# Q and K computed with tokens on partitions and then transposed, against Q and K computed transposed

## The chip, the core and the metric

The kernel runs on one core of a Trainium2 chip, in one launch, on float32 data. The metric is the device time of that launch in microseconds (us). Its engines are named as in the profile: PE is TensorE (PEld its weight loads), DVE is VectorE, ACT is ScalarE, POOL is GpSimd, and SP issues the DMAs.

## The reference

The input x is 4 sequences of 512 tokens with 1024 features. One block of attention and one feed-forward block are computed, each between two layer norms, with a residual:

```
x = x + layernorm(attention(layernorm(x)))
x = x + layernorm(ffn(layernorm(x)))

attention: qkv = x @ w_qkv.T + b_qkv      # 32 query heads, 8 key/value heads, 32 wide
           q, k = rope(q), rope(k)        # pairs (even, odd) turned by the token's angle
           attn = softmax(causal(q @ k.T / sqrt(32)))
           out  = (attn @ v) @ w_o.T + b_o
ffn:       top 2 of 8 experts by x @ gate_w.T, softmax over the two
           x @ base_w.T + base_b + 2 * sum over experts of weight * (x @ A_e.T) @ B_e.T
```

## The kernel before

The 2048 tokens are 16 tiles of 128 tokens (`tok.t`), four to a sequence (`tok.i` is the place in the sequence). Tiles go through the stages in pairs. For each pair the program does: layer norm and transposes of x (`normed_x`, tiles `xa`, `pt_xn`, `T_xn`); K and V (`keys_values`, `acc_kv`); Q (`queries`, `acc_q`); attention in 88 groups of heads (`scores` into `sc`, softmax, `turn` into `pt_p`, `values` into `av`); the output product (`acc_o`, into `w`); a layer norm, residual (`y`) and second layer norm, transposes (`pt_h`, `T_h`); the gate and LoRA products (`acc_gl`, `pt_low`); and the base product (`acc_f`).

The three 1024-wide products (Q, output, base) of a pair of tiles are made with seven half-size products in place of eight (`seven`: sums `s1` to `s4` of the inputs, sums of the weights that are mixed once into DRAM, `mixed_q`, `mixed_o`, `mixed_f`). The weights arrive as 128x512 `piece` tiles in a ring of 14.

Q and K leave TensorE already transposed, features on partitions and tokens along the free axis. For Q that is `project_turned` (L612): for each piece four matmuls, a 128x128 block of the piece being the stationary operand and 128 tokens the moving one (L623). For K it is the first half of `keys_values` (L1014), 16 such matmuls for a tile of tokens; V takes 8 matmuls with 256 moving columns (L1023). `rotate` (L792) applies the rotary embedding in this layout: a VectorE `stream_shuffle` swaps the halves of each head (L805), VectorE multiplies by sin and GpSimd by cos (L803), VectorE adds (L817). Its cos and sin tables are transposed once on TensorE at the start (`rope_tables`, L845). Biases of Q and K are one value for each partition.

In the softmax (`softmax`, L1511), VectorE adds the causal mask (L1526) and takes the negated maximum (L1536) for two quadrants of four heads at a time; ScalarE takes the exponential with its sum (L1478); VectorE the reciprocal (L1507); GpSimd scales (L1492); TensorE transposes (`turn`, L1552), ScalarE or VectorE copies out (L330, L331), and TensorE multiplies by V (L1575).

The order on every engine is fixed when the program is built. An `Order` object holds a planned time for every step and the costs written in the code; `tensor` (L233) picks TensorE's next step among lanes (scores, transposes, values, and dense products last), and every other engine takes, among the operations planned to be ready, the one with the lowest `urgent` number. On the chip each engine then works through its list in order and waits where an operand is late. Slots limit what is in flight: 4 PSUM banks beside the four of `sc`, 8 soft-max tiles, 2 `xa`, 3 `y`, 14 pieces. All DMAs go through SP's one list.

A step's planned cost and what it needs look like this:

```
g.turned = [
    Step(0.109 * blocks, partial(turn, g, r), [g.normed[r]], bank=True)
    for r in range(QUADS)
]
```

The functions that the diff touches:

Of the kernel before, what the change touches and what calls it, by code (L numbers as in the profile page):

```python
# [33 lines left out]
SAFE = 0.6  # L34
# [44 lines left out]
class Step:  # L79


    def __init__(self, us, issue, needs=(), bank=False, soon=()):
        self.us, self.issue, self.needs = us, issue, list(needs) + list(soon)
        self.tiled = False
        self.piece = None
        self.bank, self.soon = bank, soon
        self.done = Task()


class Order:  # L90
    ENGINES = ("dve", "act", "pool", "sp")

    def __init__(self, banks):
        self.now = self.at = 0.0
        self.free = dict.fromkeys(self.ENGINES, 0.0)
        self.waiting = {e: [] for e in self.ENGINES}
        self.seq = 0
        self.banks = banks

# [133 lines left out]
    def tensor(self, scores, urgent, values, dense):  # L233


        while True:
# [11 lines left out]
            us = steps[0].us + TILING * steps[0].tiled  # L248
            if lane is scores and values and values[0].tiled and self._is_ready(values[0]):
                steps.append(values.pop(0))  # L250
                us = steps[0].us + steps[1].us + PAIRED
# [9 lines left out]
def kernel(  # L261
# [27 lines left out]
    BANKS, SOFT, RING = 4, 8, 14  # L289
# [6 lines left out]
    kvpool = ctx.enter_context(tc.tile_pool(name="kvpool", bufs=2))  # L296
# [12 lines left out]
    qT_slots, kT_slots, raw_slots, turn_slots = Slots(8), Slots(2), Slots(2), Slots(2)  # L309
    xa_slots, y_slots, w_slots, v_slots = Slots(2), Slots(3), Slots(4), Slots(8)  # L310
# [54 lines left out]

    bqk_sb = const.tile([P, ND + NKT], F32, name="bqk_sb")
    bv_sb = const.tile([P, KVD], F32, name="bv_sb")
    cos_sb = const.tile([P, NQ, P], F32, name="cos_sb")
    sin_sb = const.tile([P, NQ, P], F32, name="sin_sb")
# [13 lines left out]
    def loads(what):  # L383
# [16 lines left out]
    biases = {"q": bqk_sb, "o": bo_sb, "f": bbase_sb}  # L400
    bias_steps = {
        name: const.tile([P, ND // 2 if name == "q" else 512], F32, name=f"bias_step_{name}")
        for name in plain
    }
    has_bias = {name: Task() for name in plain}
# [38 lines left out]
    def bias_step(name):  # L444
        yield loaded["b", name]
        b, n = biases[name], bias_steps[name].shape[1]
        yield combine(
            4, lambda: bias_steps[name], lambda: b[:, n : 2 * n], lambda: b[:, :n], ALU.subtract
# [115 lines left out]
    def transposes(dst, src, halves, name, slot):  # L564
# [3 lines left out]
        for h in range(NH):  # L568
# [17 lines left out]
            steps.append(Step(0.44, issue, [halves[h], slot], bank=True))  # L586
# [25 lines left out]
    def project_turned(x, w, name, needs, take):  # L612


        acc = []
        steps = []

        def issue(c):
            if not acc:
                acc.append(ps.tile([P, 4, P], F32, tag="ps", name=f"acc_{name}"))  # L620
            last = c == len(needs) - 1
            for f in range(4):
                nc.tensor.matmul(  # L623
                    acc[0][:, f, :],
                    lhsT=w(c)[:, f * P : (f + 1) * P],
                    rhs=x(c),

                    start=(c == 0 and f == 0),
                    stop=last,
                    skip_group_check=True,  # L630
                )
            if last:
                start(take(acc[0], steps_of[c].done), order.now)

        for c in range(len(needs)):
            steps.append(Step(0.872, partial(issue, c), needs[c], bank=(c == 0)))
        steps_of = list(steps)
        return steps

# [6 lines left out]
    def whole(name, tok_name, k, lhsT, ready, take, room, used=None, more=None):  # L646


# [5 lines left out]
        if name == "q":  # L654
            return with_pieces(
                used,
                project_turned(
                    lambda c: lhsT()[:, c, :],
                    lambda c: used[c].sb,
                    f"{name}_{tok_name}_{k}",  # L660
                    needs,
                    take,
                ),
            )
# [14 lines left out]
    def seven(name, pair_name, tiles, ready, out, room, ended, free, more=None):  # L679
# [33 lines left out]

        def bias(what):
            if name == "q":
                return lambda: what[:, :H].unsqueeze(2).to_broadcast([P, H, P])
            return lambda: what[:, :512]

# [13 lines left out]
            (bias(biases[name]), c11, None),  # L732
            (c11, c21, None),
            (c11, c11, None),
            (bias(bias_steps[name]), c22, None),
# [7 lines left out]
        def take(k, acc, when):  # L743
# [12 lines left out]
            yield dve(0.69, 0, lambda: nc.vector.tensor_add(to(), acc, in1()))  # L756
# [9 lines left out]
        for k, (lhs, wants, of, h, half) in enumerate(blocks):  # L766
# [11 lines left out]
            def w(c, used=used, extra=extra):  # L778
                return used[c].sb if c < H else extra[1]

            label, end = f"{name}_{pair_name}_{k}", partial(take, k)
            steps += with_pieces(
                used,
                project_turned(lhsT, w, label, needs, end)
                if name == "q"
                else project(lhsT, w, 512, label, needs, end),
# [3 lines left out]
    SWAP = [(d + HD // 2) % HD for d in range(HD)]  # L790

    def rotate(raw, out, i, name):  # L792


        n = raw.shape[1]
        yield turn_slots.take()
        turn = ropes.tile([P, 4, P], F32, tag="turn", bufs=2, name=f"turn_{name}")[:, :n, :]
        cos, sin = (
            a[:, i, :].unsqueeze(1).to_broadcast([P, n, P]) for a in (cos_sb, sin_sb)
        )  # L800

        def multiply(t, by, engine):
            engine.tensor_tensor(out=t, in0=t, in1=by, op=ALU.mult)  # L803

        yield dve(0.1 + n * 0.135, 2, lambda: nc.vector.stream_shuffle(turn, raw, SWAP))  # L805

        def by_cos():
            yield pool(0.2 + n * 0.27, 1, partial(multiply, raw, cos, nc.gpsimd))

        has_cos = start(by_cos(), order.at)  # L810
        yield [loaded["sin"]]
        yield dve(0.1 + n * 0.145, 2, partial(multiply, turn, sin, nc.vector))
        yield has_cos
        yield dve(
            0.1 + n * 0.155,
            2,
            lambda: nc.vector.tensor_tensor(out=out(), in0=raw, in1=turn, op=ALU.add),  # L817
        )
        turn_slots.give(order.at)

    def rope_tables():

        def table(at, name, to):
            wide, has_wide = [], Task()

            def widen():
                yield loaded["rope"]
                yield turn_slots.take()  # L830

                def issue():
                    wide.append(ropes.tile([P, 4, P], F32, tag="turn", bufs=2, name=f"wide_{name}"))
                    nc.gpsimd.tensor_copy(
                        wide[0].rearrange("p i (r d) -> p i r d", d=HD)[:, :NQ],
                        rope_sb[:, :, at, :].unsqueeze(2).to_broadcast([P, NQ, QUADS, HD]),
                    )

                yield pool(0.9, 1, issue)
                has_wide.finish(order.at)  # L840

            def turn_table():
                pt = ps.tile([P, 4, P], F32, tag="ps", name=f"pt_{name}")
                for i in range(NQ):
                    nc.tensor.transpose(pt[:, i, :], wide[0][:, i, :], ident)  # L845

                def end():
                    yield step.done
                    turn_slots.give(order.at)
                    yield act(  # L850
# [963 lines left out]
```

## Time and profile before

| | |
|---|---|
| median of 3 runs | 1201.9 us (1200.41 to 1201.95) |
| profiled execution: its own time | 1199.83 us |
| its span, first to last instruction | 1197.7 us |
| mean granted TensorE clock | 0.992 |
| busy PE / DVE / POOL / ACT | 1144.1 / 865.8 / 638.4 / 497.1 us |
| TensorE's first instruction after the span's start | 7.49 us |
| TensorE's last matmul begins | 1187.56 us |

The span lies 2.1 us below the execution's own time, and that execution 2.1 us below the median. In the timeline a row gives the start, the time until the last of its instructions ends, engine, line, operation, output and inputs, and the number of instructions; float32 matmuls appear as two instructions each, transposes as one. Since matmuls are pipelined, the cost of a row in a run without idle time is the start of the next row less its own start.

### The profile page before, as it was taken

Reading aid. Unit: us, or ns where it says so; the run is one execution under the profiler, and the core shown is the slowest. Engines: PE = TensorE matmul, PEld = TensorE weight load, DVE = VectorE, ACT = ScalarE, POOL = GpSimd, SP = SyncE. Lnnn points to the kernel's source line nnn. Section 1 sums busy time; section 2 is a strip of 40 time slices with the busy share of each in tenths; the row PEclk is TensorE's granted clock in tenths of the full one; section 3 lists DMA queues with packets and bytes.
Section 4 is the critical chain, followed back from the end, with each engine's and each line's share of the span. In section 5 each row is a group of like instructions: output and inputs, shape, how many; then the busy total and the mean of one; then the engine's idle time right before and its main releaser. Section 6 shows DMA issues by size and latency. Waiting matters only on the chain.

```text
span 1197.7 us, 24865 instructions
## 1 busy us (share of the span) xinstructions
PE 1144.1 (96%) x8976; PEld 796.1 (66%) x8976; DVE 865.8 (72%) x1704; ACT 497.1 (42%) x1447; POOL 638.4 (53%) x874
## 2 busy tenths in 40 slices
PE   6999899999799999999999999999999999979996
PEld 6988757875468855687658885577855875545443
DVE  4787878886677866888677886677766796777353
ACT  1335344543445344454345544444444533454110
POOL 2566857653656545555376654555555563554321
PEclk9999999999999999999999999999999999999999
DMA  9568769555572547715587234761558545733783
GB/s 325 207 237 303 262 227 317 206 180 168 185 232 88 175 157 246 214 66 165 158 260 231 93 124 142 254 208 47 172 187 277 178 150 177 255 106 119 250 304 102
DMA packets 119626, 232.10 MB, mean 194 GB/s; under 512 B 14800, under 2 KB 15952, under 8 KB 119504
## 3 DMA queue, kind: packets, MB, share of 16 engines
q1 hardware_dynamic: 119504, 230.51, 58.7%
q8 instruction: 72, 1.18, 0.4%
q14 instruction: 50, 0.41, 0.1%
HBM read 209.49 MB, written 20.97 MB: 192 GB/s over the span
## 4 chain that ended last, share of the span: by engine, by line
PE 75%; DVE 10%; POOL 7%; ACT 3%; issue 2%; DMA 2%; SPq 0%; POOLq 0%; ACTq 0%; DVEq 0%
PE acc_f L600 18%; PE acc_o L600 15%; PE acc_q L623 12%; PE pt_p L1552 10%; PE sc L1457 6%; PE av L1575 5%; POOL pr L1492 3%; DVE nmax L1536 3%; PE acc_kv L1014 3%; PE acc_kv L1023 3%; ACT pr L1478 2%; PE acc_gl L600 2%; POOL qT L803 1%; DVE sc L1526 1%; PE pt_xn L575 1%
## 5 line engine op out<-in xcount | busy, mean ns | idle before, releaser
L1492 POOL TENSOR_SCALAR pr<-pr,rtot 128x256 f32<-128x256 f32 (+3 forms) x512 | 304.1, 609 | 266.6 <-DVE rtot L1507 208.2
L1478 ACT ACTIVATE pr<-sc,nmax 128x256 f32<-128x256 f32 (+3 forms) x512 | 264.7, 531 | 204.8 <-DVE nmax L1536 96.6
L1536 DVE TENSOR_REDUCE nmax<-sc 128x2 f32<-128x768 f32 (+3 forms) x176 | 198.0, 1125 | 61.4 <-ACT pr L1478 60.0
L330 ACT COPY prT<-pt_p 128x512 f32<-128x512 f32 (+1 forms) x206 | 109.4, 543 | 227.1 <-PE pt_p L1552 226.3
L1552 PE MATMUL pt_p<-ident,pr 128*128 128x128 f32 x1280 | 180.4, 278 | 18.8 <-POOL pr L1492 13.7
L1552 PEld LDWEIGHTS pt_p<-ident,pr 128*128 128x128 f32 x1280 | 143.1, 140 | 70.2 <-issue 33.1
L331 DVE COPY prT<-pt_p 128x512 f32<-128x512 f32 (+1 forms) x146 | 94.0, 645 | 40.6 <-PE pt_p L1552 39.2
L623 PE MATMUL acc_q<-T_xn,piece 128*128 128x128 f32 x896 | 108.7, 278 | 2.1 <-DMA piece<-in_w_qkv_dram 2.1
L600 PE MATMUL acc_f<-piece,T_h 128*128 128x512 f32 x232 | 109.7, 598 | 0.4 <-ACT prT L330 0.4
L623 PEld LDWEIGHTS acc_q<-T_xn,piece 128*128 128x128 f32 x896 | 105.7, 195 | 5.7 <-issue 5.3
L623 PE MATMUL acc_q<-s_q,piece 128*128 128x128 f32 x896 | 109.0, 276 | 0.4 <-ACT prT L330 0.3
L600 PE MATMUL acc_o<-piece,s_o 128*128 128x512 f32 x224 | 103.5, 601 | 3.6 <-POOL s_o L338 3.6
L1478 ACT ACTIVATION_READ_ACCUMULATOR pr<-sc,nmax 128x1 f32 x512 | 106.0, 207 | 0.0
L623 PEld LDWEIGHTS acc_q<-s_q,piece 128*128 128x128 f32 x896 | 104.4, 192 | 1.5 <-ACT prT L330 0.8
L600 PE MATMUL acc_o<-piece,aT 128*128 128x512 f32 x232 | 104.4, 593 | 0.0
L600 PE MATMUL acc_f<-piece,s_f 128*128 128x512 f32 x224 | 103.6, 594 | 0.4 <-POOL s_f L338 0.4
L1526 DVE TENSOR_TENSOR sc<-sc,cmask 128x256 f32<-128x256 f32 (+2 forms) x176 | 96.4, 548 | 10.4 <-ACT pr L1478 5.3
L1575 PEld LDWEIGHTS av<-prT,v 128*32 128x32 f32 x2560 | 65.3, 110 | 51.6 <-issue 42.1
L1457 PE MATMUL sc<-kT,qT 32*128 32x384 f32 (+3 forms) x1024 | 93.9, 464 | 0.6 <-DVE qT L817 0.5
L1575 PE MATMUL av<-prT,v 128*32 128x128 f32 x2560 | 90.4, 276 | 1.3 <-ACT prT L330 1.0
L338 POOL TENSOR_TENSOR y<-y,w 128x512 f32<-128x512 f32 x62 | 78.8, 1286 | 22.6 <-ACT w L550 19.9
L525 POOL TENSOR_TENSOR rstd<-veps,neg_half 128x1 f32<-128x1 f32 x64 | 36.8, 579 | 101.3 <-DVE veps L521 100.3
(159 smaller groups left out, 1522.6 us busy)
## 6 DMA issues: line engine op xcount, KB each, us to landing
piece<-in_w_o_dram SPq DMA_DIRECT2D x116, 256.0 KB, 3.9
piece<-in_w_base_dram SPq DMA_DIRECT2D x116, 256.0 KB, 3.2
piece<-mixed_q SPq DMA_DIRECT2D x112, 256.0 KB, 3.7
piece<-mixed_o SPq DMA_DIRECT2D x112, 256.0 KB, 4.1
piece<-mixed_f SPq DMA_DIRECT2D x112, 256.0 KB, 3.2
piece<-in_w_qkv_dram SPq DMA_DIRECT2D x100, 256.0 KB, 3.8
xa<-in_x_dram SPq DMA_DIRECT2D x32, 256.0 KB, 3.4
y<-in_x_dram SPq DMA_DIRECT2D x16, 512.0 KB, 5.1
```

The costliest lines, as they stand in the source:

```text
L330: act=(0.15 + n * 0.00085, lambda: nc.scalar.copy(out(), in_())),
L331: dve=(0.15 + n * 0.00105, lambda: nc.vector.tensor_copy(out(), in_())),
L338: engine.tensor_tensor(out=out(), in0=in0(), in1=in1(), op=op)
L600: nc.tensor.matmul(acc[0][:, :n], lhsT=lhsT(c), rhs=w(c), start=(c == 0), stop=last)
L623: nc.tensor.matmul(acc[0][:, f, :], lhsT=w(c)[:, f * P : (f + 1) * P], rhs=x(c),  start=(c == 0 and f == 0), stop=last, skip_group_check=True,
L1457: nc.tensor.matmul(sc[:, r, c * n : (c + 1) * n], lhsT=tok.qT[g.kt][rows, (g.at + c) % GROUP, :], rhs=seq.kT[rows, g.kt, :n], start=True, ...
L1478: lambda: nc.scalar.activation(pr[:, c * n : (c + 1) * n], sc4[:, r, c, :], AF.Exp, bias=nmax[:, r, c : c + 1], accum_out=total[:, r, c : ...
L1492: lambda: nc.gpsimd.tensor_scalar(pr[:, c * n : (c + 1) * n], pr[:, c * n : (c + 1) * n], rtot[:, r, c : c + 1], 1.0, ALU.mult, ALU.mult,),
L1526: lambda: nc.vector.tensor_tensor(out=diag, in0=diag, in1=cmask.unsqueeze(1).unsqueeze(1).to_broadcast([P, q, g.n, P]), op=ALU.add,),
L1536: lambda: nc.vector.tensor_reduce(nmax[:, some, : g.n], sc4[:, some], AX.X, ALU.max, negate=True),
L1552: nc.tensor.transpose(pt[:, j, :], g.pr[r][:, j * P : (j + 1) * P], ident)
L1575: nc.tensor.matmul(av[r * HD : (r + 1) * HD, c, :], lhsT=g.seq.v[j][:, head * HD : (head + 1) * HD], rhs=g.prT[r][:, c * (i + 1) + j, :], ...
```

## The change

Q and K are now computed as the other products are: 128 tokens are the stationary operand and 512 columns of weights (for K and V together, 512 columns of `wkv_sb`) the moving one. The result has tokens on partitions. The bias becomes a row that is broadcast to all partitions (`bqkv_sb`, 768 KB of DMA in place of a small one and 128 KB). `rotate` works in this layout, with the halves of a head swapped by addressing: two VectorE multiplications by sin, one of GpSimd by cos, one VectorE addition. Then TensorE transposes: four 128x128 blocks for each Q tile of 512 columns (32 tiles, `pt_q`), two for each K tile (16 tiles, `pt_k`), and ScalarE (Q, with the scale) or ScalarE or VectorE (K) copies out. The two table transposes at the start are gone, and so is the shuffle.

To make room for six `raw` tiles, `xa` has one buffer in place of two, `y` two in place of three, the ring 13 pieces in place of 14; K has four separate tiles.

In the order, the turn of an even quadrant now waits in the plan until the odd one beside it is scaled too; masks and maxima have urgency 0 (1 before) and the sums that take a product of `seven` out of PSUM have urgency 1 (0 before). The planner adds 0.05 us where transposes follow other work, and its margin `SAFE` is 0.3 in place of 0.6. The diff, cut to its core (removed bodies stand in the functions above):

```diff
-SAFE = 0.6
+TURNING = 0.05
+SAFE = 0.3
...
+            us += TURNING * (steps[0].turns and not self.turned)
+            self.turned = steps[0].turns
...
-    BANKS, SOFT, RING = 4, 8, 14
+    BANKS, SOFT, RING = 4, 8, 13
...
-    kvpool = ctx.enter_context(tc.tile_pool(name="kvpool", bufs=2))
+    kvpool = ctx.enter_context(tc.tile_pool(name="kvpool", bufs=4))
...
-    qT_slots, kT_slots, raw_slots, turn_slots = Slots(8), Slots(2), Slots(2), Slots(2)
-    xa_slots, y_slots, w_slots, v_slots = Slots(2), Slots(3), Slots(4), Slots(8)
+    qT_slots, kT_slots, raw_slots, turn_slots = Slots(8), Slots(4), Slots(6), Slots(1)
+    xa_slots, y_slots, w_slots, v_slots = Slots(1), Slots(2), Slots(4), Slots(8)
...
-    bqk_sb = const.tile([P, ND + NKT], F32, name="bqk_sb")
-    bv_sb = const.tile([P, KVD], F32, name="bv_sb")
-    cos_sb = const.tile([P, NQ, P], F32, name="cos_sb")
-    sin_sb = const.tile([P, NQ, P], F32, name="sin_sb")
+    bqkv_sb = const.tile([P, QKV], F32, name="bqkv_sb")
...
-            steps.append(Step(0.44, issue, [halves[h], slot], bank=True))
+            steps.append(Step(0.44, issue, [halves[h], slot], bank=True, turns=True))
...
-    def project_turned(x, w, name, needs, take):
...
-            yield dve(0.69, 0, lambda: nc.vector.tensor_add(to(), acc, in1()))
+            yield dve(0.69, 1, lambda: nc.vector.tensor_add(to(), acc, in1()))
...
-                project_turned(lhsT, w, label, needs, end)
-                if name == "q"
-                else project(lhsT, w, 512, label, needs, end),
+                project(lhsT, w, 512, f"{name}_{pair_name}_{k}", needs, partial(take, k)),
...
-    def rotate(raw, out, i, name):
...
+    def rotate(raw, n, i, name):
+        nh, half = n // HD, HD // 2
         yield turn_slots.take()
+        turn = ropes.tile([P, 512], F32, tag="turn", name=f"turn_{name}")
+        raw3, turn3 = (a[:, :n].rearrange("p (h d) -> p h d", d=HD) for a in (raw, turn))
+        for a, b in ((0, half), (half, 0)):
+            sin = rope_sb[:, i, 1, a : a + half].unsqueeze(1).to_broadcast([P, nh, half])
+            yield dve(
+                0.1 + n * 0.00065,
+                2,
+                lambda: nc.vector.tensor_tensor(
+                    out=turn3[:, :, a : a + half],
+                    in0=raw3[:, :, b : b + half],
+                    in1=sin,
+                    op=ALU.mult,
+                ),
+            )
+        cos = rope_sb[:, i, 0, :].unsqueeze(1).to_broadcast([P, nh, HD])
+        yield pool(
+            0.2 + n * 0.0021,
+            1,
+            lambda: nc.gpsimd.tensor_tensor(out=raw3, in0=raw3, in1=cos, op=ALU.mult),
         )
         yield dve(
+            0.1 + n * 0.0012,
             2,
+            lambda: nc.vector.tensor_add(raw[:, :n], raw[:, :n], turn[:, :n]),
         )
         turn_slots.give(order.at)
-    def rope_tables():
...
+    def new_raw(name):
+        return ropes.tile([P, 512], F32, tag="raw", bufs=6, name=f"raw_{name}")
...
-        job.xn = xpool.tile([P, D], F32, tag="xa", bufs=2, name=f"xa_{job.name}")
+        job.xn = xpool.tile([P, D], F32, tag="xa", bufs=1, name=f"xa_{job.name}")
...
-            tok.y = xpool.tile([P, D], F32, tag="y", bufs=3, name=f"y_{tok.t}")
+            tok.y = xpool.tile([P, D], F32, tag="y", bufs=2, name=f"y_{tok.t}")
...
+        def take(acc, done):
+            yield done
             job.read(order.at)
+            yield loaded["b", "q"]
             def v_issue():
                 seq.v[i] = kvpool.tile([P, KVD], F32, tag="v", bufs=8, name=f"v_{t}")
+                nc.vector.tensor_add(
+                    seq.v[i], acc[:, KVD : 2 * KVD], bqkv_sb[:, D + KVD : D + 2 * KVD]
+                )
             yield dve(0.41, 0, v_issue)
+            seq.has_v[i].finish(order.at)
+            raw.append(new_raw(f"k_{t}"))
+            yield dve(
+                0.1 + KVD * 0.00115,
+                0,
+                lambda: nc.vector.tensor_add(
+                    raw[0][:, :KVD], acc[:, :KVD], bqkv_sb[:, D : D + KVD]
+                ),
+            )
             banks.give(order.at)
+            yield from rotate(raw[0], KVD, i, f"k_{t}")
+            k_ready.finish(order.at)
+        def turn_k():
+            pt = ps.tile([P, 4, P], F32, tag="ps", name=f"pt_k_{t}")
+            for kt in range(NKT):
+                nc.tensor.transpose(pt[:, kt, :], raw[0][:, kt * P : (kt + 1) * P], ident)
+            def end():
+                yield step_k.done
+                raw_slots.give(order.at)
+                for kt in range(NKT):
+                    yield copy(
+                        P,
+                        lambda: seq.k_tile(kt)[:, i * P : (i + 1) * P],
+                        lambda: pt[:, kt, :],
+                    )
+                banks.give(order.at)
+                seq.has_k[i].finish(order.at)
+            start(end(), order.now)
+        step_k = Step(0.23, turn_k, [k_ready], bank=True, turns=True)
+        needs = [[job.ready[c // 4], loaded["kv", c]] for c in range(ND)]
+        needs[0] += [has_raw]
+        products = project(
+            lambda c: job.xnT()[:, c, :], lambda c: wkv_sb[:, c, :], 2 * KVD, f"kv_{t}", needs, take
+        )
+        return [step_k], products
...
+        def ended(k, h):
+            yield from rotate(raw[k, h], 512, pair[k].i, f"q_{pair[k].t}_{h}")
+            q_ready[k, h].finish(order.at)
+        def turn_q(k, h):
             tok = pair[k]
+            pt = ps.tile([P, 4, P], F32, tag="ps", name=f"pt_q_{tok.t}_{h}")
+            for c in range(4):
+                nc.tensor.transpose(pt[:, c, :], raw[k, h][:, c * P : (c + 1) * P], ident)
+            def end():
+                yield steps_q[k, h].done
+                raw_slots.give(order.at)
                 tok.qT[h] = qpool.tile([P, 4, P], F32, tag="qT", name=f"qT_{tok.t}_{h}")
+                yield act(
+                    0.6, 0, lambda: nc.scalar.activation(tok.qT[h], pt, AF.Copy, scale=QSCALE)
+                )
+                banks.give(order.at)
+                tok.has_q[h].finish(order.at)
+            start(end(), order.now)
+        for k, h in [(0, 0), (0, 1), (1, 0), (1, 1)][: NH * len(pair)]:
+            q_ready[k, h] = Task()
+            steps_q[k, h] = Step(0.44, partial(turn_q, k, h), [q_ready[k, h]], bank=True, turns=True)
+        names = [q_job[tok] for tok in pair]
         if len(pair) == 2:
...
+            return [[steps_q[0, 0], steps_q[0, 1]], [steps_q[1, 1]], [steps_q[1, 0]]], steps
...
                     0.15 + q * g.n * 0.135,
-                    1,
+                    0,
...
                     0.15 + q * g.n * n * 0.00105,
-                    1,
+                    0,
...
+        bias_q = load(("b", "q"), 768, bqkv_sb, b_qkv.broadcast_to([P, QKV]))
...
-            yield from loads([rotary] + biases_qkv)
+            yield from loads([bias_q, rotary])
...
-            Step(0.109 * blocks, partial(turn, g, r), [g.normed[r]], bank=True)
+            Step(0.109 * blocks, partial(turn, g, r), [g.normed[r | 1]], bank=True, turns=True)
```

## The prediction

> **What bounds the kernel now.** I read first the page's busy times, its chain that ended last, and busy time by stretches of the span, then TensorE's timeline, then the groups by shape.
>
> ```profile
> PE 1144.1 (96%) x8976; PEld 796.1 (66%) x8976; DVE 865.8 (72%) x1704; ACT 497.1 (42%) x1447; POOL 638.4 (53%) x874
> ...
> PE 75%; DVE 10%; POOL 7%; ACT 3%; issue 2%; DMA 2%; SPq 0%; POOLq 0%; ACTq 0%; DVEq 0%
> ```
>
> TensorE is the bound: 1144.1 of 1197.7 us. Of the other 53.6 us, 7.5 pass before its first instruction and about 9 after its last matmul (1187.56 plus 1.02 us); some 37 us are waits between. So two numbers decide: how much TensorE work the change adds, and what becomes of the 37. Stretches of the span (length, then busy time of PE, PEld, DVE, ACT, POOL, then the granted clock):
>
> ```profile
> 50.00:160.00 110.00, 100.42 (x985) 87.24 (x983) 90.48 (x151) 46.14 (x152) 81.39 (x103) 1.00 0.68 237
> 310.00:330.00 20.00, 13.64 (x144) 7.96 (x139) 12.39 (x22) 11.09 (x43) 14.44 (x22) 0.91 0.51 172
> 1055.00:1100.00 45.00, 36.67 (x325) 24.30 (x317) 34.63 (x71) 22.31 (x68) 24.41 (x39) 0.92 0.24 74
> 1073.00:1076.00 3.00, 1.55 (x6) 1.18 (x7) 1.93 (x7) 2.96 (x17) 2.09 (x5) 0.50 0.00 0
> 1076.00:1079.00 3.00, 3.00 (x10) 2.08 (x10) 0.96 (x2) 1.33 (x8) 3.00 (x6) 0.50 0.00 0
> ```
>
> The waits sit in three places: 9.6, 6.4 and 8.3 us, 24 of the 37. The last two rows show a second cost: after the longest wait the clock is granted at 0.50 for 6 us, which loses 3 us more. TensorE's timeline:
>
> ```profile
> 321.71 5.40 PE L600 MATMUL acc_o<-piece,s_o 128*128 128x512 f32 x8 [3.61 <-POOL s_o L338]
> 326.94 1.45 PE L600 MATMUL acc_o<-piece,aT 128*128 128x512 f32 x3
> ...
> 399.77 3.74 PE L623 MATMUL acc_q<-T_xn,piece 128*128 128x128 f32 x32
> 403.34 1.88 PE L600 MATMUL acc_f<-piece,T_h 128*128 128x512 f32 x4
> ...
> 413.06 2.84 PE L1014 MATMUL acc_kv<-T_xn,wkv_sb 128*128 128x128 f32 x24
> 415.74 1.89 PE L1023 MATMUL acc_kv<-wkv_sb,T_xn 128*128 128x256 f32 x8
> ...
> 1044.52 1.96 PE L1552 MATMUL pt_p<-ident,pr 128*128 128x128 f32 x16
> 1046.32 7.03 PE L600 MATMUL acc_o<-piece,s_o 128*128 128x512 f32 x16
> ...
> 1073.67 1.08 PE L575 MATMUL pt_h<-ident,w 128*128 128x128 f32 x4 [4.94 <-DVE w L544]
> ...
> 1180.69 7.03 PE L600 MATMUL acc_f<-piece,T_h 128*128 128x512 f32 x16
> 1187.56 1.02 PE L600 MATMUL acc_f<-wlora_sb,lowT 128*128 128x512 f32 x2
> ```
>
> Start to start in unbroken runs: a 512-column matmul (two instructions) takes 2 x 6.87/16 = 0.859 us. The 128-column Q form takes 3.57/32 = 0.112 us an instruction, 0.893 us for the eight of a piece. A transpose takes 1.80/16 = 0.1125 us. The eight instructions at 321.71 take 5.23 us in place of 3.44: 1.8 us lost to the slower clock after a wait.
>
> **TensorE work, part by part.** Q has 228 pieces (2 tiles x 16, then 7 pairs x 28). In the new form each saves 0.893 - 0.859 = 0.034 us: 7.8 us. K and V of a tile: now 32 instructions of 0.112 (2.68/24) and 16 V instructions of 0.216 (the first tile's V: 3.45 us from 20.23 to 23.68 for 16), 7.03 us; after, eight matmuls of 0.859, 6.87. Over 16 tiles: 2.6 us saved. Added: 32 x 4 + 16 x 2 = 160 transposes, less 8 of the tables, 152 x 0.1125 = 17.1 us. In the changed program's fixed order on TensorE, 73 scores are followed directly by values, 77 before; a break costs about 0.1 us more: 0.4. Sum: 17.1 - 7.8 - 2.6 + 0.4 = 7.1 us more work on the bound. No other engine can hide it.
>
> One rule weighs on this. The row says 0.1125 us for a transpose, at a granted clock of 1.00. The Trainium skill (TensorE: Matmul & The Clock Gate, Part 4) says that transposes do not count as activity for the clock gate and gives about 275 ns for one in a kernel; by that the 152 would cost 42 us and the change would lose some 32. Its figure equals the page's mean length of one transpose record, which is not the spacing; the row decides.
>
> **The other engines.** Groups by shape (mean ns after the busy time):
>
> ```profile
> L805 DVE STREAM_SHUFFLE turn_q<-qT 128x512 f32<-128x512 f32 x32 | 23.4, 733 | 0.0
> L803 DVE TENSOR_TENSOR turn_q<-turn_q,sin_sb 128x512 f32<-128x512 f32 x32 | 31.7, 994 | 0.3
> L1478 ACT ACTIVATION_READ_ACCUMULATOR pr<-sc,nmax 128x1 f32 x512 | 106.0, 207 | 0.0
> L1478 ACT ACTIVATE pr<-sc,nmax 128x128 f32<-128x128 f32 x128 | 45.1, 385 | 24.1 <-DVE nmax L1536 13.8 <-DVE sc L1526 10.3
> ```
>
> VectorE per Q tile loses a shuffle (0.733) and a full multiplication (0.994) and gains two of half the size: 0.35 each if dense, 0.62 (K's 256-element multiplication, 624 ns) if the strided form is slow; I take 0.5. That is 0.7 x 32 = 23 us less on VectorE (15 to 33); K adds a 0.42 bias sum and two copies of about 0.28, some 10 us back. ScalarE gains 32 copies of 0.59 and loses 32 of 0.37. At 72% and 42% busy both stay off the bound, so these count nothing by themselves. GpSimd's cos product stays at 1.475 us.
>
> **The waits.** The order of TensorE's instructions is fixed in both programs, so I counted the TensorE work (at the spacings above) that stands between a producer and its consumer. Before, each big wait is where that cover is short. Near 312 us: 7.4 us from a group's scores to its first turn, then no work between the last `av` and the product that needs `s_o`. Near 149 to 156 us: 5.5 and 8.2 us from scores to turn. Near 1063 us: 6.3 and 7.0. After, the shortest such cover anywhere is 7.9 us, most are 8.6 to 13, and `s_o` has 6.1 us. What it must cover, for a 512-wide group: mask 0.43, maximum 1.22, two exponentials at 0.69 + 0.21, reciprocal 0.16, scaling 0.76: 4.4 us, up to about 9 where VectorE and ScalarE are shared. So:
> - 310 to 330 us: 6.4 + 1.8 us now, 0.6 left: -7.6.
> - 50 to 160 us: 9.6 now. The first groups (one block of keys) stay short: 16 exponentials of 0.385 + 0.207 are 9.5 us, and their cover is 14.4 and 15.5 against 14.2 and 16.8. Others gain 1 to 5 us of cover. 5 left: -4.6.
> - 1055 to 1100 us: 8.3 + 3 now. The last such group has 11.5 us of cover, where the same kind waited at 14.2; and the first `pt_h` behind it needs ScalarE after its exponentials. 8 left: -3.3.
> - Start: the 2.07 us wait for the first piece of Q goes, since K and V's weights, loaded ahead, are used first; the 768 KB bias row (2.4 us at the 322 GB/s of that stretch) delays later pieces: -1.
> - New: 48 turns of Q and K, each behind a VectorE and GpSimd chain. For K it is 0.42 + 0.42 + two products + 0.81 + 0.57, about 3 to 3.5 us, and the cover is 3.6 to 4.3 at five of 16; for Q 4.5 to 6 us with covers of 5.2 up: 0 to 10 us, near the low end: +1.8.
>
> Three edits I cost at nothing. Masks ahead of sums: a sum (0.69) waits at most 1.65 us behind them, with its PSUM bank and whoever needs that; uncovered, a few tenths each. Turns in twos: the first turn starts one scaling (0.45 to 0.76) later under dense work, and the second is 0.45 later than it need be, which is what GpSimd's lateness (13.7 us over 17 waits at L1552) is made of; gain 0 to 7, counted above. Fewer buffers: a tile's x can be asked for only after the turns of the one before, in SP's one list, with pieces behind it; the shortest distance is 10.2 us of TensorE work against about 8 for load, statistics and scaling; 0 to 3 us lost once.
>
> Sum: -7.6 - 4.6 - 3.3 - 1 + 1.8 = -14.7 of waits, +7.1 of work: -7.6. On the profiled execution 1199.8 - 7.6 = 1192.2; it lies 2.1 below the median, so 1194.3 against 1201.9.
>
> **Rivals.**
> *Slower:* the new turns themselves. TensorE works in order, so a turn that comes before its rotated tile stops everything behind it. At 0.8 us (the mean wait at L1552 on GpSimd) over half of the 48, 19 us come back, and 1194.3 - 1.8 + 19 = 1211. It decides from a mean of about 0.25 us over all 48 (12 us), where the gain is gone. For: VectorE's products share time with GpSimd (0.994 against the 0.69 of single rows early on). Against: nearly all covers exceed the chains. Chance 0.31, centred at 1208.
> *No change:* the order covers better but late engines move the waits, 8 of the 14.7 us are found: 1201. Chance 0.11.
> *Better:* the last stretch clears as well and turns cost nothing: 1184. Chance 0.10.
> *Forecast as reckoned:* 0.48, 1188 to 1199.
>
> **The numbers.** 0.2% of 1201.9 is 2.4 us, about what a measurement of this kernel can tell from no change. Faster (under 1199.5): 0.48 + 0.10 = 0.58. Within: 0.11. Slower (over 1204.3): 0.31. The range runs from 1184, the better case, to 1211, the slower rival's price; beyond lie some 2 in 10.
>
> **What would show it.** Right: TensorE's busy time up by 5 to 9 us, PE idle between its first and last matmul near 22 us, no stretch with a lowered clock between 100 and 1000 us, `acc_q` at 0.43 us an instruction. Wrong: idle above 32 us; many waits at `pt_q` or `pt_k` on VectorE's last addition; waits on DMA in the first 100 us; a transpose spacing far over 0.1125.

## The result and the profile after

The changed kernel takes 1189.0 us (median of 4 runs, 1187.5 to 1189.7) against 1201.9: a ratio of 0.9892, 95% interval 0.9875 to 0.9910. The profiled execution took 1187.52 us with a span of 1185.7, 12.0 us less than before. The direction was forecast, and the time lies in the range as reckoned, 5 us below its middle.

The page after, busy times and the chain that ended last:

```profile
PE 1145.5 (97%) x7248; PEld 627.0 (53%) x7248; DVE 823.9 (69%) x1609; ACT 533.1 (45%) x1555; POOL 608.0 (51%) x857
...
PE 80%; DVE 8%; DMA 4%; POOL 4%; ACT 2%; issue 1%; SPq 0%; POOLq 0%; ACTq 0%; DVEq 0%
```

TensorE's share of the chain rises from 75% to 80%. VectorE is busy 42 us less, three times the 13 that the prediction had, which will matter below. The same stretches as before (length, busy time of PE, PEld, DVE, ACT, POOL, then the granted clock):

```profile
50.00:160.00 110.00, 103.15 (x693) 56.58 (x694) 84.47 (x148) 54.38 (x171) 75.50 (x104) 1.00 0.76 266
310.00:330.00 20.00, 19.29 (x112) 10.63 (x113) 14.66 (x19) 12.26 (x47) 15.25 (x26) 1.00 0.70 220
1055.00:1100.00 45.00, 38.67 (x261) 23.71 (x260) 27.99 (x66) 14.47 (x50) 20.45 (x35) 0.92 0.43 143
```

At 310 to 330 us TensorE idled 6.4 us before and 0.7 now, and the clock stays at 1.00. In the other two places 6.9 and 6.3 us are left, of 9.6 and 8.3. The waits that remain, in TensorE's timeline:

```profile
59.05 0.63 PE L996 MATMUL pt_q<-ident,raw_q 128*128 128x128 f32 x4 [1.51 <-DVE raw_q L771]
...
317.04 3.67 PE L602 MATMUL acc_o<-piece,s_o 128*128 128x512 f32 x8 [0.71 <-PE av L1490]
...
1070.61 2.23 PE L577 MATMUL pt_h<-ident,w 128*128 128x128 f32 x8 [5.90 <-DVE rtot L1422]
```

The product with `s_o` now waits 0.71 us, not 3.61; one long wait, near 1070 us, is still there; and some of the new turns of Q wait for VectorE's last addition (1.51 us here, 1.27 at 107.36).

For sums over the whole span I count as **work** each row of TensorE's timeline at the spacing of its kind in unbroken runs (0.430 us for an instruction with 512 columns, 0.110 for a transpose, and so on) with what a change of kind costs; what is left between starts is **waits**, the loss to a slow clock included. Before: 1124.3 work, 56.6 waits. After: 1132.0 and 37.3. With 0.5 us less ahead of the first instruction, that is 7.7 - 19.3 - 0.5 = -12.1, the 12.0 of the span. How the sum is split depends on what is counted as a change of kind: with the commonest spacing of each pair of instructions every kernel has 13 to 16 us less work and as much more waits, and differences to the kernel before move by up to some 2 us.

### The profile page after: what moved, and what is told of

Read it like the earlier page. It is cut to its first block, busy times and chain, and to the rows that moved or that the text cites. A ratio compares the mean times of both kernels' runs of the same rounds, so it can differ in the third digit from the quotient of the medians.

```text
span 1185.7 us, 21412 instructions
## 1 busy us (share of the span) xinstructions
PE 1145.5 (97%) x7248; PEld 627.0 (53%) x7248; DVE 823.9 (69%) x1609; ACT 533.1 (45%) x1555; POOL 608.0 (51%) x857
## 4 chain that ended last, share of the span: by engine, by line
PE 80%; DVE 8%; DMA 4%; POOL 4%; ACT 2%; issue 1%; SPq 0%; POOLq 0%; ACTq 0%; DVEq 0%
PE acc_f L602 19%; PE acc_o L602 15%; PE acc_q L602 11%; PE pt_p L1467 11%; PE acc_kv L602 7%; PE sc L1372 6%; PE av L1490 6%; PE acc_gl L602 2%; DVE nmax L1451 2%; POOL pr L1407 2%; ACT pr L1393 1%; PE pt_h L577 1%; DVE sc L1441 1%; DMA mix_o<-in_w_o_dram 1%; PE pt_q L996 1%
## 5 line engine op out<-in xcount | busy, mean ns | idle before, releaser
L1467 PE MATMUL pt_p<-ident,pr 128*128 128x128 f32 x1280 | 174.2, 276 | 3.5 <-POOL pr L1407 1.6
L335 ACT COPY prT<-pt_p 128x512 f32<-128x512 f32 (+1 forms) x264 | 135.2, 548 | 83.6 <-PE pt_p L1467 82.9
L602 PE MATMUL acc_kv<-wkv_sb,T_xn 128*128 128x512 f32 x256 | 119.4, 600 | 0.0
L335 ACT COPY aT<-av 128x128 f32<-128x128 f32 (+2 forms) x82 | 25.6, 312 | 195.0 <-PE av L1490 195.0
L1393 ACT ACTIVATION_READ_ACCUMULATOR pr<-sc,nmax 128x1 f32 x512 | 108.9, 213 | 0.0
L602 PE MATMUL acc_q<-piece,s_q 128*128 128x512 f32 x224 | 105.1, 597 | 1.2 <-DVE raw_q L713 0.9
L602 PE MATMUL acc_q<-piece,T_xn 128*128 128x512 f32 x224 | 102.7, 594 | 0.0
L336 DVE COPY prT<-pt_p 128x512 f32<-128x512 f32 (+1 forms) x88 | 56.2, 641 | 32.2 <-PE pt_p L1467 31.5
```

What stands on the lines that cost most here:

```text
L335: act=(0.15 + n * 0.00085, lambda: nc.scalar.copy(out(), in_())),
L336: dve=(0.15 + n * 0.00105, lambda: nc.vector.tensor_copy(out(), in_())),
L602: nc.tensor.matmul(acc[0][:, :n], lhsT=lhsT(c), rhs=w(c), start=(c == 0), stop=last)
L1393: lambda: nc.scalar.activation(pr[:, c * n : (c + 1) * n], sc4[:, r, c, :], AF.Exp, bias=nmax[:, r, c : c + 1], accum_out=total[:, r, c : ...
L1467: nc.tensor.transpose(pt[:, j, :], g.pr[r][:, j * P : (j + 1) * P], ident)
```

## The experiments

The change has two halves: the new layout of Q and K, with its buffers, and three edits of the order: masks and maxima ahead of sums ("masks", which is two urgencies: masks and maxima from 1 to 0, and sums from 0 to 1), turns in twos ("twos"), and the planner's costs ("margin": `SAFE`, with the 0.05 of `TURNING` in the kernels with 0.3 or 0.4 except e11). In the expectations theory A is that the order's edits make the gain and the layout costs time; theory B that the layout makes it. All times are medians of 4 to 10 runs, against 1202.4, 1202.5 and 1202.7 us for the kernel before in the three sessions. Work and waits are those of each profiled execution.

| kernel | layout | order edits | time, us | ratio to before, 95% | work | waits |
|---|---|---|---|---|---|---|
| before | old | none | 1201.9 | 1 | 1124.3 | 56.6 |
| e12 | old | margin 0.5 | 1200.0 | 0.9968 to 0.9993 | 1124.6 | 58.3 |
| e11 | old | margin 0.3 | 1204.0 | 1.0003 to 1.0027 | 1125.1 | 63.6 |
| e10 | old | twos | 1204.2 | 0.9999 to 1.0022 | 1123.5 | 62.4 |
| e5 | old | masks | 1185.1 | 0.9845 to 0.9875 | 1124.5 | 44.4 |
| e8 | old | masks, margin 0.3 | 1177.7 | 0.9776 to 0.9809 | 1124.4 | 36.8 |
| e1 | old | masks, margin 0.3, twos | 1187.0 | 0.9863 to 0.9893 | 1126.3 | 42.4 |
| e2 | new | none | 1207.4 | 1.0028 to 1.0065 | 1131.0 | 55.4 |
| e4 | new | margin 0.3, twos | 1192.7 | 0.9911 to 0.9959 | 1131.4 | 40.0 |
| e6 | new | masks, twos | 1189.6 | 0.9874 to 0.9928 | 1131.3 | 37.7 |
| e3 | new | masks, margin 0.3 | 1181.7 | 0.9819 to 0.9850 | 1130.7 | 31.6 |
| e9 | new | masks, margin 0.4 | 1188.6 | 0.9857 to 0.9895 | 1131.2 | 39.7 |
| after | new | masks, margin 0.3, twos | 1189.0 | 0.9875 to 0.9910 | 1132.0 | 37.3 |
| e7 | new | as after, Q's turns doubled | 1196.0 | 0.9927 to 0.9960 | 1145.3 | 31.7 |

### The two halves apart

**e1: the order's edits on the kernel before.** Edits to its program, all three (the lines by which the planner adds `TURNING` left out):

```diff
-SAFE = 0.6
+TURNING = 0.05
+SAFE = 0.3
...
-            yield dve(0.69, 0, lambda: nc.vector.tensor_add(to(), acc, in1()))
+            yield dve(0.69, 1, lambda: nc.vector.tensor_add(to(), acc, in1()))
...
                     0.15 + q * g.n * 0.135,
-                    1,
+                    0,
...
                     0.15 + q * g.n * n * 0.00105,
-                    1,
+                    0,
...
-            Step(0.109 * blocks, partial(turn, g, r), [g.normed[r]], bank=True)
+            Step(0.109 * blocks, partial(turn, g, r), [g.normed[r | 1]], bank=True, turns=True)
```

> The kernel before with the three edits of the order alone (turns in twos, masks and maxima ahead of the sums of the seven products, the planner's margin 0.3 and 0.05 per turn); Q and K stay computed transposed, buffers as before. Theory A, the order edits took the waits away and the layout only costs 7.3 us of TensorE work: the waits fall by about 19 us as in the changed kernel and the work stays, so 1182 us. Theory B, the layout took the waits away (VectorE is 42 us less busy), the order edits are worth little: 1199 to 1203. Theory C, every new plan moves the waits by some us without a single cause: anywhere from 1188 to 1206.

**e2: the new layout with the order of before.** The same lines taken back in the changed kernel (margin 0.6, no `TURNING`, masks 1, sums 0, `g.normed[r]`):

```diff
-TURNING = 0.05
-SAFE = 0.3
+TURNING = 0.0
+SAFE = 0.6
...
-            Step(0.109 * blocks, partial(turn, g, r), [g.normed[r | 1]], bank=True, turns=True)
+            Step(0.109 * blocks, partial(turn, g, r), [g.normed[r]], bank=True, turns=True)
```

> The changed kernel with the three order edits undone: layout and buffers of the change, order rules of before. Theory A: work up by 7.3 us, waits as before: 1209 us. Theory B: the waits stay low: 1187 to 1191. Theory C: 1188 to 1206, and not the mirror image of the first run.

Measured: 1187.0 and 1207.4. The order's edits alone bring the whole gain; the layout alone is slower by 0.3 to 0.65%. Theory B falls. The layout's long wait is where it was; stretches and timeline of e2:

```profile
310.00:330.00 20.00, 15.61 (x132) 9.66 (x129) 11.09 (x16) 8.68 (x37) 14.53 (x25) 0.85 0.44 141
```

```profile
308.84 0.83 PE L1467 MATMUL pt_p<-ident,pr 128*128 128x128 f32 x4 [1.95 <-POOL pr L1407]
309.60 2.09 PE L1372 MATMUL sc<-kT,qT 32*128 32x128 f32 x32
...
319.76 5.21 PE L602 MATMUL acc_o<-piece,s_o 128*128 128x512 f32 x8 [3.61 <-POOL s_o L343]
```

It is the wait of before to the digit, 3.61 us for `s_o`.

### Which of the order's edits

**e3: without twos**, and **e4: without masks**, each from the changed kernel:

```diff
-            Step(0.109 * blocks, partial(turn, g, r), [g.normed[r | 1]], bank=True, turns=True)
+            Step(0.109 * blocks, partial(turn, g, r), [g.normed[r]], bank=True, turns=True)
```

> The changed kernel with turns planned one quadrant at a time again. If the twos carry part of the gain: TensorE's waits for GpSimd at the turns of the probabilities go from 1.7 us back towards 13.7, so 1195 to 1201. If they carry none: 1187 to 1191. Theory C: within 6 us of 1189 on either side with the change in waits spread over the span.

```diff
-            yield dve(0.69, 1, lambda: nc.vector.tensor_add(to(), acc, in1()))
+            yield dve(0.69, 0, lambda: nc.vector.tensor_add(to(), acc, in1()))
...
                     0.15 + q * g.n * 0.135,
-                    0,
+                    1,
...
                     0.15 + q * g.n * n * 0.00105,
-                    0,
+                    1,
```

> The changed kernel with masks and maxima at urgency 1 and the sums of the seven products at urgency 0 again. If masks first carry part of the gain: scores wait longer for VectorE, waits return where the cover is short, 1193 to 1200. If none: 1187 to 1191.

Measured: 1181.7 without twos, outside all its expectations, and 1192.7 without masks. Taken out of the changed kernel, masks cost 3.7 us and twos gain 7.3; both are within the scatter between orders that e9 shows below, so neither is clear from these two runs. And 3.7 us is far from the 18 that the three make in this layout, so the next runs took them one at a time in the old one.

**e5: masks alone on the kernel before.**

```diff
-            yield dve(0.69, 0, lambda: nc.vector.tensor_add(to(), acc, in1()))
+            yield dve(0.69, 1, lambda: nc.vector.tensor_add(to(), acc, in1()))
...
                     0.15 + q * g.n * 0.135,
-                    1,
+                    0,
...
                     0.15 + q * g.n * n * 0.00105,
-                    1,
+                    0,
```

> The kernel before, with only the urgencies changed: masks and maxima first, sums behind them. Theory A (the three order edits each have an effect of their own, and the effects add up): masks first took 3.7 us off the changed kernel, so 1198 to 1199 here against 1202. Rival N (any edit of a planned cost or an urgency gives a new order whose time is a draw with a scatter of several us): anything from 1195 to 1209, with no relation to the 3.7.

Measured: 1185.1, 17 us less, far outside either expectation: masks alone bring more than the whole change does. The stretch of 310 to 330 us, and TensorE's timeline there:

```profile
310.00:330.00 20.00, 19.88 (x165) 10.98 (x164) 13.99 (x25) 11.76 (x46) 18.91 (x35) 1.00 0.78 257
```

```profile
312.32 1.17 PE L1457 MATMUL sc<-kT,qT 32*128 32x128 f32 x32
...
316.22 1.02 PE L600 MATMUL acc_f<-wlora_sb,lowT 128*128 128x512 f32 x2
...
317.95 3.60 PE L600 MATMUL acc_o<-piece,aT 128*128 128x512 f32 x8
...
322.49 3.70 PE L600 MATMUL acc_o<-piece,s_o 128*128 128x512 f32 x8
```

No wait is left. TensorE's order itself is another one: dense `acc_f` work is still in hand until 317 us, while before it was used up at 306, and only output products and groups of heads followed up to 331. The timeline of before, there:

```profile
305.04 1.02 PE L600 MATMUL acc_f<-wlora_sb,lowT 128*128 128x512 f32 x2
305.89 3.60 PE L600 MATMUL acc_o<-piece,aT 128*128 128x512 f32 x8
```

The urgencies thus moved far more than VectorE's list. They also moved work between engines. The groups that copy the turned soft-max out of PSUM, before and then e5 (the number after x is the count):

```profile
L330 ACT COPY prT<-pt_p 128x512 f32<-128x512 f32 (+1 forms) x206 | 109.4, 543 | 227.1 <-PE pt_p L1552 226.3
L331 DVE COPY prT<-pt_p 128x512 f32<-128x512 f32 (+1 forms) x146 | 94.0, 645 | 40.6 <-PE pt_p L1552 39.2
```

```profile
L331 DVE COPY prT<-pt_p 128x512 f32<-128x512 f32 (+1 forms) x84 | 53.4, 638 | 35.8 <-PE pt_p L1552 34.8
```

With masks first, the planner gives 62 more of these copies to ScalarE, and VectorE's time in them falls by 41 us. VectorE as a whole loses 24 (865.8 to 842.0), since it takes over other work: the additions of L338 on it go from 90 to 120, and GpSimd is busy 31 us less. The split of the copies goes with masks in every kernel: VectorE makes 81 to 93 of them in the eight kernels with masks first, and 144 to 156 in the six without. In the changed kernel this group is 38 us shorter on VectorE (94.0 to 56.2), which is most of the 42.

**e6: the changed kernel with the planner's costs of before.**

```diff
-TURNING = 0.05
-SAFE = 0.3
+TURNING = 0.0
+SAFE = 0.6
```

> The changed kernel with the planner's costs of before (margin 0.6 in place of 0.3, no 0.05 for the first turn); masks first and turns in twos stay. Theory A, adding up: all order edits together are worth 18 us in the new layout, masks first 3.7 of them, twos cost 7, so the margin is worth about 21: 1208 to 1212. Rival N: 1185 to 1200. If waits grow, they should be waits of TensorE for VectorE at the places 310 to 330 and 1055 to 1100 us.

Measured: 1189.6. Margin and `TURNING` do nothing beside masks and twos; adding up fails.

**e8: masks and margin on the kernel before.** Against e1:

```diff
-            Step(0.109 * blocks, partial(turn, g, r), [g.normed[r | 1]], bank=True, turns=True)
+            Step(0.109 * blocks, partial(turn, g, r), [g.normed[r]], bank=True)
```

> The kernel before (Q and K made transposed) with masks first and the planner's new costs, but without turns in twos. Theory A, adding up: 1187 with all three, less the 7 us that twos cost in the new layout: 1178 to 1182, the shortest of all, since the layout's 152 transposes are not there. Rival N: 1182 to 1195. Rival L (the new layout is what makes the order without twos good): above 1187.

Measured: 1177.7, the fastest of all, 11 us under the changed kernel. It keeps the old layout, and its waits (36.8) are as few as the changed kernel's. Against e1 it has no twos, and its soft-max turns don't carry the planned 0.05.

**e10: twos alone on the kernel before; e11: margin 0.3 alone; e12: margin 0.5 alone.**

```diff
-            Step(0.109 * blocks, partial(turn, g, r), [g.normed[r]], bank=True)
+            Step(0.109 * blocks, partial(turn, g, r), [g.normed[r | 1]], bank=True)
```

> The kernel before, with turns in twos alone. Theory A (twos cost time by themselves): 1207 to 1212. Rival S (twos and masks first stand in for each other: either takes away the waits where VectorE is late, and together they give little more): 1188 to 1196.

```diff
-SAFE = 0.6
+SAFE = 0.3
```

> The kernel before, with the planner's margin 0.3 in place of 0.6 and nothing else. Theory A (masks first is what the gain needs; the margin only adds to it): 1198 to 1204. Rival S2 (the margin alone takes away the long waits): 1188 to 1196, and no wait near 310 to 330 us.

```diff
-SAFE = 0.6
+SAFE = 0.5
```

> The kernel before with the margin at 0.5 in place of 0.6: an order made anew from nearly the same costs, which measures the scatter between orders. Theory A: 1200 to 1205, so that differences of 7 us and more between kernels mean something. Rival N (every order is a draw): as far as 1190 or 1210.

Measured: 1204.2, 1204.0, 1200.0: e10 in neither of its expectations, e11 and e12 in those of theory A. Four orders of the old layout without masks lie within 4.2 us; three with masks lie at 1177.7, 1185.1 and 1187.0. The step between the two sets is larger than the scatter in either, so in the old layout masks are the cause: alone (e5) and with the others (e1, e8) they bring the gain, and without them twos and margin, each alone, do not. e12's timeline still shows the wait for `s_o`, a little later:

```profile
329.38 5.95 PE L600 MATMUL acc_o<-piece,s_o 128*128 128x512 f32 x8 [3.61 <-POOL s_o L338]
```

**e9: e3 with margin 0.4.**

```diff
-SAFE = 0.3
+SAFE = 0.4
```

> The changed kernel without turns in twos, and with the planner's margin at 0.4 in place of 0.3, to give another order of the same kind. Theory A (turns in twos cost 7 to 9 us, whatever the order): 1179 to 1185, near the 1181.7 of margin 0.3. Rival N (the 7 us are a lucky order): 1186 to 1192.

Measured: 1188.6, where 0.3 gave 1181.7, as rival N expected. A change of 0.1 in a planned margin moves the time by 7 us, as much as taking twos out did. Twos cost 7 us (after against e3), 9.3 (e1 against e8, with the 0.05), and 1.5 or nothing in e10; whether that is twos or the scatter between orders stays open.

### The price of the transposes

**e7: each of Q's transposes made twice**, the plan being the same:

```diff
-            for c in range(4):
+            for c in [0, 1, 2, 3, 0, 1, 2, 3]:
                 nc.tensor.transpose(pt[:, c, :], raw[k, h][:, c * P : (c + 1) * P], ident)
```

> The changed kernel with each of Q's 128 transposes made twice in a row, the second over the first (the planned order is unchanged). Theory A (the new transposes lie on the path of TensorE at 0.11 us each): 128 x 0.1104 = 14.1 us more, 1203. Rival W (TensorE would wait at these places anyway for the rotated tile or a bank, so that transposes are partly free): less than 8 us more, under 1197. By the Trainium skill's figure of some 275 ns for a transpose it would be 35 us, 1224.

Measured: 1196.0, 7.0 us more for 128 transposes, half of what they take, and so under the 8 us of rival W. The work is there (128 at 0.109 us, start to start, are 14.0 us; 13.3 more in the table), but waits fall from 37.3 to 31.7; of the fall 3.6 us are idle time ahead of the turns of Q and K (8.5 to 4.9). One such place, in e7's timeline, beside the first row of after's shown above:

```profile
58.67 1.06 PE L996 MATMUL pt_q<-ident,raw_q 128*128 128x128 f32 x8 [0.46 <-DVE raw_q L771]
```

The wait of 1.51 us has become 0.46. Behind two doubled turns TensorE comes to this place 0.67 us later (58.21 in place of 57.54), and VectorE had that much more time; the tile was also ready 0.38 us sooner, which the run does not explain. So the work added here cost its length less the waits that it covered later. The layout points the same way in the table: at equal order edits it adds about 6 to 7 us of work, but only 5.0 (before, e2), 4.0 (e8, e3) and 2.0 us (e1, after) of time. These are differences between orders too, and within their scatter.

## Why the prediction was right, and where it was not

| step | predicted | measured in the profiled executions, counted by spacing |
|---|---|---|
| TensorE work | +7.1 | +7.7 |
| 310 to 330 us | -7.6 | -8.1 |
| 50 to 160 us | -4.6 | -4.1 |
| 1055 to 1100 us | -3.3 | -3.5 |
| start | -1 | -2.5 |
| all other waits, the new turns among them | +1.8 | -1.5 |
| sum | -7.6 | -12.0 |

**Work.** Right within 0.6: Q's products at 0.43 us an instruction, transposes at 0.11, and 128 transposes doubled cost 0.055 us each in time and 0.11 in work (e7). The Trainium skill's some 275 ns for a transpose (TensorE: Matmul & The Clock Gate, Part 4) would have made that 35 us; the measurement decides against it. (The prediction's loss of 32 us by this figure is its work alone; with the 14.7 us of waits it would have been 17.) Nor does its other statement hold here, that transposes don't count as activity: in e4 TensorE ran nothing but 16 transposes, 3.14 us of work, from 1075.86 to 1079.27 at a clock of 0.50, and then the clock was 1.00.

TensorE's busy time, which I had named as the sign (5 to 9 us more), rose by 1.4 only. It also counts what the lowered clock adds, by an estimate 3.0 us less after than before (half of the 5.8 and 11.9 us of its busy time at 0.50); the other 3 us of the difference stay open. It was a poor sign, and start-to-start spacing the better one. The other signs came: 24.0 us idle between the first and the last matmul (22 named), no lowered clock between 100 and 1000 us, `acc_q` at 0.43 us an instruction.

**The three places.** Counted by spacing, each is within 0.6 us of the forecast. The forecast itself was made in idle time and loss to the clock, and in these the stretches shown lose 7.5, 2.7 and 2.0 us (5.7 idle and 1.8 of the clock; 2.7; 2.0, at a clock of 0.92 before and after): only the first is near. And from 50 to 160 us the agreement is luck in either count. The soft-max turns, whose cover I had counted, wait 8.5 us there before and 1.7 after, more of a gain than the 4.6 that I took; the new turns wait 4.9 us in the same stretch, where I had put 1.8 for all of them, in a row of its own. The two errors cancel. These turns between 50 and 162 us, in before, e5, e2 and after (busy, mean ns, then idle time ahead of them):

```profile
L1552 PE MATMUL pt_p<-ident,pr 128*128 128x128 f32 x120 | 19.4, 283 | 8.5 <-POOL pr L1492 8.5
L1552 PE MATMUL pt_p<-ident,pr 128*128 128x128 f32 x126 | 20.2, 287 | 8.1 <-POOL pr L1492 8.1
L1467 PE MATMUL pt_p<-ident,pr 128*128 128x128 f32 x113 | 16.2, 280 | 0.6 <-POOL pr L1407 0.6
L1467 PE MATMUL pt_p<-ident,pr 128*128 128x128 f32 x116 | 16.6, 278 | 1.7 <-POOL pr L1407 1.3 <-ACT qT L1003 0.4
```

The covers were read from the changed program's fixed order, which held all edits at once.

**The cause.** Here a step failed: "Three edits I cost at nothing. Masks ahead of sums: a sum (0.69) waits at most 1.65 us behind them". I priced what the edit does to two neighbours in VectorE's list. The urgency is an input of the planner, and with it the order of TensorE and the split of copies between engines change; e5 shows the edit to be worth 17 us alone. The covers that I counted held its work with that of the other edits, and the sum came out because they were counted, not because the edit was understood. The places do not all belong to it: at 310 to 330 us masks alone leave no wait (e5) and the layout alone leaves 3.61 us for `s_o` (e2), but at 50 to 162 us masks alone leave the soft-max turns at 8.1 us and the layout alone at 0.6 (there a wait of 5.2 us of the scores for ScalarE comes in their place). VectorE's relief was likewise put on the wrong account: the layout alone (e2) takes 8 us off it, and some 15 if the ten more copies that it makes there are left out, near my 13 (a half product took 0.53 us there for my 0.5); most of the 42 is copies.

**Turns in twos** ("gain 0 to 7, counted above"): the wait that I meant does go: TensorE waits 6.9 us for GpSimd's scaling in e8 and 0.7 in e1. The time does not: work and waits together are 7.5 us more in e1. In no pair of runs here did this edit gain time.

**The missing 5 us.** The gain at the start was under-sized by 1.5. The new turns' +1.8 was under-sized too: they did wait, and more than I allowed: 8.5 us of idle time in these two groups of after (busy, mean ns, then idle time ahead of them), of which 6.2 on VectorE's last addition:

```profile
L996 PE MATMUL pt_q<-ident,raw_q 128*128 128x128 f32 x128 | 19.6, 277 | 6.9 <-DVE raw_q L771 4.6 <-DVE rank L1163 1.3 <-DVE rtot L1422 0.9
L945 PE MATMUL pt_k<-ident,raw_k 128*128 128x128 f32 x32 | 6.4, 283 | 1.6 <-DVE raw_k L771 1.6
```

That is 0.18 us on a mean turn, under the 0.25 from which the slower rival would have decided. What I had left out is on the other side: the soft-max turns wait 3.5 us in all, and 18.8 before, over the whole span and not in three places alone; between 600 and 1055 us all waits together fall by 5.7. The groups, before and after:

```profile
L1552 PE MATMUL pt_p<-ident,pr 128*128 128x128 f32 x1280 | 180.4, 278 | 18.8 <-POOL pr L1492 13.7 <-ACT prT L330 1.9 <-DVE T_xn L331 1.3
```

```profile
L1467 PE MATMUL pt_p<-ident,pr 128*128 128x128 f32 x1280 | 174.2, 276 | 3.5 <-POOL pr L1407 1.6 <-DVE prT L336 0.4 <-ACT qT L1003 0.4
```

**The rivals.** The slower one described a true mechanism at a third of its price. The better one (1184) expected the last stretch to clear; it did not, in any kernel. That the layout alone is slower was in none of them: no rival took the two halves apart. So the time was right, and the gain was credited to a change whose larger half costs time.

**Open.** Masks alone in the new layout were not run, nor the two urgencies of "masks" one without the other. And e4, without masks, is still 14.7 us faster than e2, so in that layout twos and margin stand in for them in part; how, the runs do not show. Whether masks work by VectorE's order, by the copies or by TensorE's order is not separated either: the planner changes all three.

## What to carry to other kernels

Where a planner builds the order, a number in it is no local edit: run it alone on the old kernel before crediting its gain to the change that came with it, and run two or three neighbours of it to learn the scatter between orders (here some 4 to 7 us). Count waits from the finished order of the changed program, and look at who waits in a stretch as well as how long: one of the three counts here was right by two errors that cancelled. Price added work on the bound at its length less the waits that it covers later (14 us cost 7 in e7). Here the layout is the half to leave out: the old one with masks first and the smaller margin takes 1177.7 us, 2.1% less than before (interval 1.9 to 2.2%); a neighbouring order may lie some us off that.

## What was not expected of the hardware

- **The clock changed on a fixed grid, so the place of a wait on it counted.** In e2 the wait of 1.95 us at 308.84 is followed by 32 score matmuls in 2.02 us start to start (309.60 to 311.62), with a granted clock of 0.57 from 308.8 to 311.6. Before, 1.89 us at 312.39 is followed by the same 32 in 1.10 us (312.98 to 314.08), at a clock of 1.00. In each of the 14 traces all changes of the granted clock lie whole steps of 3.41 us apart (before: at 321.88, 325.29 and, 149 steps behind the first, 830.46). On this grid e2's wait lies in one step, which holds 1.46 us of TensorE work, and the next step runs at 0.50; the wait of before is cut in two by a border at 311.64, its steps hold 2.27 and 2.66 us, and the clock stays. Two steps of e2, then two of before:

```profile
305.78:309.19 3.41, 1.46 (x36) 1.17 (x36) 2.72 (x7) 2.12 (x6) 1.10 (x2) 1.00 0.95 299
309.19:312.60 3.41, 3.41 (x40) 2.86 (x39) 0.33 (x3) 0.58 (x1) 2.36 (x5) 0.50 0.38 145
308.23:311.64 3.41, 2.27 (x35) 1.01 (x34) 2.32 (x6) 1.92 (x5) 0.00 (x0) 1.00 0.70 200
311.64:315.05 3.41, 2.66 (x44) 2.25 (x44) 1.32 (x6) 1.56 (x5) 3.31 (x6) 1.00 0.64 250
```

Over all traces, their first 9 and last 14 us left out, a step at 1.00 was followed by one at 0.50 in 42 cases, with at most 1.76 us of TensorE work in it, and by one at 1.00 in 4639, with at least 1.47. The Trainium skill (TensorE: Matmul & The Clock Gate, Part 1) says that the activity is watched in a free-running window; the steps of these traces agree with that.

- **GpSimd's product with cos was slower for what ran beside it, and not for its form.** With 128x512 elements in each case it takes 1.285 us on the mean with tokens on partitions and took 1.475 with features on them, where cos was broadcast over another axis. But the medians are alike (min/median/max, ns, before and after):

```profile
L803 POOL TENSOR_TENSOR qT<-qT,cos_sb x32: 1260/1279/1781, 30.8 to 984.6; 128x512 f32<-128x512 f32 x32
L766 POOL TENSOR_TENSOR raw_q<-raw_q,rope_sb x32: 1264/1272/1695, 27.8 to 988.2; 128x512 f32<-128x512 f32 x32
```

Before, 15 of the 32 took 1.6 to 1.8 us, and 14 of these ran while VectorE multiplied by sin. After, the product with cos overwrites the tile that VectorE's products read and starts behind them, and one of the 32 took more than 1.3 us.
